# Layer 0 attention: scores on four row groups, masked into SBUF, softmax in SBUF, transposes four steps behind, one copy in three on VectorE

## The chip, the cores and the metric

The kernel runs on one NeuronCore of a Trainium2 chip. The metric is the device time of one execution in microseconds; less is better. Five engines take part: TensorE (PE; its weight loads are shown apart as PEld), VectorE (DVE), ScalarE (ACT), GpSimd (POOL) and SyncE (SP, which only issues transfers here). Each engine runs its own queue in order, and semaphores order the engines among each other.

## The reference

The model is two transformer layers with the normalisation after each block. All data is fp32. Layer 0 is grouped-query attention with 32 heads of 16 channels and 8 key/value heads, causal, on 4 sequences of 256 tokens and 512 channels, and a feed-forward product whose weight is dequantised. Layer 1 is attention with 32 heads of 128 channels and a distance bias, and a product with a weight of -1, 0 and 1.

```python
# layer 0, cut
q = (x @ Wq + bq).reshape(B, S, 32, 16).transpose(0, 2, 1, 3)
k = repeat(4, (x @ Wk + bk) as 8 heads of 16)
v = repeat(4, (x @ Wv + bv) as 8 heads of 16)
scores = einsum('bhqd,bhkd->bhqk', q, k) / sqrt(16)
scores = where(causal, scores, -1e9)
p = softmax(scores, axis=-1)
out = einsum('bhqk,bhkd->bhqd', p, v) @ Wo + bo
x = layernorm(x + out)
x = layernorm(x + x @ dequantised_weight.T + bias)
# layer 1: the same shape of block, with its own weights
```

## The kernel before

Tokens lie in eight tiles of 128. Layer 0 is one software pipeline, the function `run`. It goes over 64 steps `(b, qt, h, i)`: batch `b` (4), query tile `qt` (2), `h` (2) and `i` (4). A step is four heads of one query tile. For `qt` 0 the keys are the first 128 tokens, so the scores of a step are 128 x 4 x 128 ("first half" of a batch, eight steps); for `qt` 1 they are all 256 ("second half").

Queries and keys are held with channels on the partitions, in strips of 32: strip r holds two key/value heads of 16 channels. `kT` has two copies of the keys, in each of which one of the two heads of every strip is zeroed (index `e`), so that a matmul over the 32 partitions of a strip gives the scores of one head only. `i` counts the four query heads that share a key head.

`begin0` starts a step. It multiplies on two strips (rows 64h to 64h+63), each against both copies of the keys, into a PSUM tile of two banks; the pool `ps_s0` has two such tiles. DVE adds the causal mask in place to the 128 columns on the diagonal (L489), for all four heads at once, and takes the negated maxima over all columns (L492). ACT makes four exponentials, one a head, out of PSUM into the SBUF tile `pr`, with the row sums beside them (L276). Then `divide0` is called: the reciprocal of the sums of the step before on DVE (L281), and the division of its `pr` on POOL (L284).

Three steps later `transpose0` transposes `pr` on PE (L299), one bank for each 128 keys, and `evacuate` copies the bank to the tile `prT`. `evacuate` takes turns: one copy on DVE (L102), the next on ACT (L104). Two steps after the transposes `end0` is called. It does nothing until the last of the eight steps of a query tile; then it multiplies all the probabilities with the values (L532; 8 matmuls for `qt` 0, 16 for `qt` 1) into the bank `o`, four strips of output columns at a time, copies `o` to `oT` and appends a generator `tail0` to the list `tails`.

Between the steps, `fill` advances other work by one piece: `project0` of the next batch (transposed x, keys pk L388, queries pq L401, values pv), and the open tails: output projection py (L440) with its residual sum y (L442), normalisation with statistics on DVE and a power on POOL (L262), transposed x1, feed-forward product pf (L457), second normalisation, and the transpose into `x2T` that layer 1 reads.

[...] three in the pool `ps_w`, shared by the transposes, projections and tails; four for scores (two tiles of two); one for `o`.

The order of instructions on each engine is not the order of the calls alone: a scheduler moves independent instructions, so a score step may stand inside a block of pf or pq. Instructions marked `keep_in_program_order` are held in place.

Layer 1, from about 270 us on, is bound by PE. It uses the same `evacuate`, with alternating turns.

Of the kernel before, what the change touches and what calls it, by code (L numbers as in the profile page):

```python
# [12 lines left out]
F32 = mybir.dt.float32  # L13
# [15 lines left out]
MASKED = -3.0e38  # L29
# [32 lines left out]
def block_kernel(  # L62
# [29 lines left out]
    dram = pool(ctx, "dram", 4, space=bass.MemoryType.DRAM)  # L92

    turn = [0]
    last = []

    def evacuate(dst, src):

        if not last:
            turn[0] ^= 1  # L100
        if turn[0] and not last:
            nc.vector.tensor_copy(dst, src)  # L102
        else:
            nc.scalar.copy(dst, src)  # L104
# [31 lines left out]
    def bank_m(name):  # L136
        return ps_w.tile([P, D], F32, tag="w", name=name)
# [127 lines left out]
    def normalise(dst, y, factors):  # L265
        nc.vector.tensor_scalar(dst, y, *factors, ALU.subtract, ALU.mult)
# [8 lines left out]
    def exponentials(pr, sc, nm, sums, i, w):  # L275
        nc.scalar.activation(  # L276
            pr[:, i, 0:w], sc, AF.Exp, bias=nm[:, i : i + 1], accum_out=sums[:, i : i + 1]
        )
# [193 lines left out]

    ahead, tails = deque(), deque()

    def begin0(b, qt, h, i):

        qT, kT, _ = qkv0[b]
        w = (qt + 1) * P
        name = f"0_{b}_{qt}_{h}_{i}"
        nm, sums, pr = softmax_tiles(a0, name, 6)  # L480
        sc = ps_s0.tile([P, 2, 2, 2 * P], F32, tag="s", name=f"sc_{name}")
        for j in range(2):
            rows = slice(32 * (2 * h + j), 32 * (2 * h + j) + 32)
            nc.tensor.matmul(  # L484
                sc[:, j, :, 0:w], qT[rows, i, ts(qt, P)], kT[rows, :, 0:w], start=True, stop=True
            )
        scf = sc.rearrange("p j e k -> p (j e) k")
        diag = scf[:, :, w - P : w]
        nc.vector.tensor_tensor(  # L489
            diag, diag, causal.unsqueeze(1).to_broadcast([P, G, P]), ALU.add  # L490
        )
        nc.vector.tensor_reduce(nm, scf[:, :, 0:w], AX.X, ALU.max, negate=True)  # L492
# [12 lines left out]
        if undivided:  # L505
            divided(*undivided.pop(), True)

    def transpose0(b, qt, h, i, pr):
        name = f"0_{b}_{qt}_{h}_{i}"
        if i == 0:  # L510
            open0[h] = [
                a0.tile(
                    [P, G, 4, 4, 32], F32, tag="prT", name=f"prT0_{b}_{qt}_{h}_{kt}", bufs=5
                )
                for kt in range(qt + 1)
            ]
        transposed_probabilities(
            name,
            pr,
            [(kt, open0[h][kt][:, i].rearrange("p j n q -> p n j q")) for kt in range(qt + 1)],  # L520
        )
        return open0[0], open0[1] if h else None

    def end0(b, qt, h, i, prT):
        if (h, i) != (1, G - 1):
            return
        o = ps_o0.tile([P, G * P], F32, tag="o", name=f"o0_{b}_{qt}")
        v = qkv0[b][2]
        for kt in range(qt, -1, -1):
            for e in range(2):  # L530
                for r in (2, 3, 0, 1):
                    nc.tensor.matmul(  # L532
                        o[32 * r : 32 * r + 32, :],
                        v[:, kt, r, ts(e, 32)],
                        prT[r // 2][kt][:, :, :, 2 * (r % 2) + e, :],
                        start=(kt == qt and e == 0),
                        stop=(kt == 0 and e == 1),
                    )
        oT = a0.tile([P, G, P], F32, tag="oT", name=f"oT0_{b}_{qt}")
        evacuate(oT.rearrange("p i q -> p (i q)"), o)  # L540
        tails.append(tail0(2 * b + qt, oT))

    def before0(step):
        b, qt, h, i = step
        if (qt, h, i) == (0, 0, 0):
# [14 lines left out]
    ahead.append(project0(0))  # L560
    tails.append(feed_forward_weight())
    run(
        [(b, qt, h, i) for b in range(B) for qt in range(2) for h in range(2) for i in range(G)],
        begin0,
        transpose0,
        end0,
        before0,
        fill,
        lag=3,
        more=2,  # L570
        rest=divide0,
    )
    la.close()


# [470 lines left out]
    def fill1():  # L1046
# [16 lines left out]
        lag=1,  # L1063
# [39 lines left out]
```

## Time and profile before

| what | value |
|---|---|
| time, median of 3 runs | 961.02 us (960.78 to 964.9) |
| the profiled execution | 960.96 us, span 958.8 us |
| PE busy | 922.0 us, 96% |
| DVE busy | 619.4 us, 65% |
| POOL busy | 445.6 us, 46% |
| ACT busy | 315.2 us, 33% |
| layer 0's loop | the first score matmul starts at 13.91 us; layer 1's first product starts at 270.11 us |
| score matmuls, first half | 128 records of 32x256, mean 426 ns |
| score matmuls, second half | 128 records of 32x512, mean 638 ns |
| mask L489 | 64 of 128x512, mean 694 ns |
| maxima L492 | 32 of 128x512, mean 686 ns; 32 of 128x1024, mean 1222 ns |
| exponentials L276, layer 0 | 128 of 128x128, mean 371 ns; 128 of 128x256, mean 475 ns |
| division L284, layer 0 | 32 of 128x512, mean 1112 ns; 32 of 128x1024, mean 1907 ns |

How to read it. A row of the profile names line, engine, operation, output and inputs with shapes, then the count, the busy time, the mean of one, and the idle time of the engine before these instructions with what ended it. An fp32 matmul stands as two records, and its duration includes the pipeline's depth, so that the distance between starts tells better what it costs. A share of busy time is an average over stages; what a change in one stage is worth is read from that stage. The granted clock is that of TensorE, as a part of its full speed.

### The profile page before, as it was taken

What the parts mean: (1) busy time and instruction counts of PE and PEld (TensorE: products, weight loads), DVE (VectorE), ACT (ScalarE), POOL (GpSimd) and SP (SyncE); (2) the same over time, 40 slices, a digit from 0 to 9 for tenths busy, and PEclk for the clock granted to TensorE, in tenths of its full rate; (3) what the DMA queues carried; (4) which work ended last, traced back from release to release, by engine and by line L of the source; (5) the groups of instructions that cost most, each with busy time, mean ns of one, the idle gap of its engine ahead of it and who ended that gap; (6) DMA issues with size and microseconds to landing.
All of it is one profiled execution on the core that took longest, in us unless ns stands there. A gap on an engine that the chain in (4) does not pass through costs nothing.

```text
span 958.8 us, 11377 instructions
## 1 busy us (share of the span) xinstructions
PE 922.0 (96%) x3593; PEld 554.1 (58%) x3593; DVE 619.4 (65%) x1291; ACT 315.2 (33%) x1194; POOL 445.6 (46%) x461
## 2 busy tenths in 40 slices
PE   8999999998899999999999999999999999999996
PEld 5655455553544445666666666666666666666652
DVE  4886777778533447655667666666676576666566
ACT  3674555466411003232222222212122122214441
POOL 3563553554457015445443543534543534556732
PEclk9999999999899999999999999999999999999998
DMA  8500000000020102444443353343344333432001
GB/s 242 184 1 1 0 1 1 1 1 1 1 88 22 45 0 72 128 115 126 110 135 86 112 152 99 121 125 95 117 125 111 115 83 110 126 94 69 1 34 55
DMA packets 76418, 74.45 MB, mean 78 GB/s; under 512 B 5957, under 2 KB 52678, under 8 KB 76358
## 3 DMA queue, kind: packets, MB, share of 16 engines
q1 hardware_dynamic: 75014, 72.02, 26.2%
q10 hardware_dynamic: 1344, 1.70, 0.6%
q8 instruction: 29, 0.48, 0.2%
q14 instruction: 31, 0.25, 0.1%
HBM read 49.58 MB, written 24.12 MB: 77 GB/s over the span
## 4 chain that ended last, share of the span: by engine, by line
PE 79%; POOL 9%; DVE 6%; ACT 2%; issue 1%; DMA 1%; ACTq 0%; POOLq 0%; DVEq 0%
PE p_q L632 18%; PE po L881 14%; PE sc L968 7%; PE o L1008 7%; PE p_k L632 5%; PE p_v L632 5%; PE sc L484 4%; PE pt L299 3%; PE py L440 3%; PE pf L457 3%; PE o L532 2%; PE pq L401 2%; POOL pr L284 2%; ACT pr L276 2%; PE py L842 2%; POOL x L903 2%
## 5 line engine op out<-in xcount | busy, mean ns | idle before, releaser
L276 ACT ACTIVATE pr<-sc,nm 128x256 f32<-128x256 f32 (+1 forms) x512 | 209.5, 421 | 362.2 <-DVE nm L984 277.2
L284 POOL TENSOR_TENSOR pr<-pr,sums 128x512 f32<-128x512 f32 (+1 forms) x128 | 190.4, 1489 | 231.2 <-DVE sums L281 220.9
L976 DVE SCALAR_TENSOR_TENSOR sc<-table,sc 128x128 f32<-128x128 f32 (+1 forms) x256 | 86.1, 356 | 34.7 <-PE sc L968 32.4
L276 ACT ACTIVATION_READ_ACCUMULATOR pr<-sc,nm 128x1 f32 x512 | 104.2, 203 | 0.0
L968 PEld LDWEIGHTS sc<-kT,qT 128*128 128x128 f32 x512 | 82.3, 191 | 35.1 <-issue 29.7
L968 PE MATMUL sc<-kT,qT 128*128 128x256 f32 (+1 forms) x512 | 95.0, 327 | 0.0
L1008 PE MATMUL o<-prT,v 128*128 128x512 f32 x192 | 92.9, 592 | 0.0
L310 DVE STREAM_TRANSPOSE blocks<-pr 128x512 f32<-128x512 f32 x84 | 57.6, 698 | 45.2 <-POOL pr L284 45.1
L646 DVE TENSOR_TENSOR qT<-p_q,qT 128x512 f32<-128x512 f32 x96 | 64.6, 686 | 33.6 <-PE p_q L632 32.8
L299 PE MATMUL pt<-ident,pr 128*128 128x128 f32 x432 | 64.3, 284 | 11.7 <-POOL pr L284 8.2
L299 PEld LDWEIGHTS pt<-ident,pr 128*128 128x128 f32 x432 | 50.7, 145 | 38.1 <-issue 19.9
L984 DVE TENSOR_REDUCE nm<-sc 128x2 f32<-128x512 f32 (+1 forms) x128 | 70.1, 551 | 1.5
L484 PE MATMUL sc<-kT,qT 32*128 32x256 f32 (+1 forms) x256 | 61.6, 532 | 2.8 <-ACT pr L276 2.7
L492 DVE TENSOR_REDUCE nm<-sc 128x4 f32<-128x512 f32 (+1 forms) x64 | 61.0, 954 | 1.2
L881 PE MATMUL po<-wo,so 128*128 128x256 f32 x224 | 58.0, 381 | 2.1 <-POOL so L612 2.1
L632 PE MATMUL p_q<-x2T,ws_q 128*128 128x512 f32 x128 | 59.8, 592 | 0.0
L489 DVE TENSOR_TENSOR sc<-sc,causal 128x512 f32<-128x512 f32 x64 | 44.4, 694 | 22.8 <-PE sc L484 22.5
L104 ACT COPY o<-o 128x512 f32<-128x512 f32 x29 | 17.0, 586 | 124.9 <-PE o L1008 124.9
L632 PE MATMUL p_q<-xt,ws_q 128*128 128x512 f32 x128 | 57.7, 592 | 0.0
L881 PE MATMUL po<-wo,o 128*128 128x256 f32 x224 | 57.7, 380 | 0.0
L632 PE MATMUL p_q<-x2T,wq 128*128 128x512 f32 x128 | 57.6, 592 | 0.0
L881 PE MATMUL po<-to,so 128*128 128x256 f32 x224 | 53.3, 381 | 1.0 <-POOL so L615 1.0
(155 smaller groups left out, 1410.2 us busy)
## 6 DMA issues: line engine op xcount, KB each, us to landing
way<-blocks SPq DMA_DIRECT2D x112, 128.0 KB, 2.5
prT<-way SPq DMA_DIRECT2D x28, 512.0 KB, 3.7
wq<-in_L_attn_w_qkv_dram SPq DMA_DIRECT2D x8, 1024.0 KB, 5.1
wo<-in_L_attn_w_o_dram SPq DMA_DIRECT2D x8, 1024.0 KB, 5.1
way<-blocks SPq DMA_DIRECT2D x112, 64.0 KB, 1.8
prT<-way SPq DMA_DIRECT2D x28, 256.0 KB, 2.6
wk<-in_L_attn_w_qkv_dram SPq DMA_DIRECT2D x4, 512.0 KB, 4.1
wv<-in_L_attn_w_qkv_dram SPq DMA_DIRECT2D x2, 1024.0 KB, 6.3
```

Of the source, the lines that this page charges most:

```text
L276: nc.scalar.activation(pr[:, i, 0:w], sc, AF.Exp, bias=nm[:, i : i + 1], accum_out=sums[:, i : i + 1])
L284: nc.gpsimd.tensor_tensor(pr[:, :, 0:w], pr[:, :, 0:w], sums.unsqueeze(2).to_broadcast([P, G, w]), ALU.mult)
L299: nc.tensor.transpose(pt[:, i, :], pr[:, i, ts(kt, P)], ident)
L484: nc.tensor.matmul(sc[:, j, :, 0:w], qT[rows, i, ts(qt, P)], kT[rows, :, 0:w], start=True, stop=True)
L492: nc.vector.tensor_reduce(nm, scf[:, :, 0:w], AX.X, ALU.max, negate=True)
L632: nc.tensor.matmul(bank, fixed, moving, start=(c == 0), stop=(c == 1))
L646: add = lambda dst, a, b: nc.vector.tensor_tensor(dst, a, b, ALU.add)
L881: nc.tensor.matmul(bank[:, ts(n, HALF)], left[:, c, :], right[:, c, :], start=(c == 0), stop=(c == 1),)
L968: nc.tensor.matmul(sc[:, m, 0:w], qT[:, 2 * j + m, b * S + qt * P : b * S + (qt + 1) * P], kT[:, b * S : b * S + w], start=True, stop=True,)
L976: nc.vector.scalar_tensor_tensor(sc[:, m, 0:w], table[:, 2 * P - w :], slopes[kv * G + 2 * j + m], sc[:, m, 0:w], ALU.mult, ALU.add,)
L984: nc.vector.tensor_reduce(nm[:, 2 * j : 2 * j + 2], sc[:, :, 0:w], AX.X, ALU.max, negate=True)
L1008: nc.tensor.matmul(o, v1[:, 2 * b + kt, ts(kv, P)], prT[:, kt].rearrange("p j h q -> p h j q"), start=(kt == 0), stop=(kt == qt),)
```

## The change

A step becomes `(b, qt, e, i)`: all four strips against one copy of the keys, four matmuls with 128 or 256 columns instead of two with 256 or 512. The heads of a step are others, the number of steps and of heads in a step is the same. The four matmuls write four banks, and `ps_s0` has one such tile instead of two smaller ones.

DVE adds the mask in one instruction over the whole width and writes to SBUF, into `pr`; the mask tile has 128 columns of zeros ahead of the triangle for this. The maxima and the exponentials read `pr` in SBUF, and the exponentials are made in place.

The transposes of a step come four steps behind it instead of three. `prT` is now one tile for each `e`, with both blocks of keys, and two such tiles instead of five smaller ones. The output matmuls of a query tile are made in two blocks, after the last step of each `e`, into the same bank, which stays open between them.

In layer 0 `evacuate` gives DVE one copy in three, and ACT two; from layer 1 on they alternate again.

```diff
     turn = [0]
+    shares = [3]
...
         if not last:
-            turn[0] ^= 1
-        if turn[0] and not last:
+            turn[0] += 1
+        if turn[0] % shares[0] == 1 and not last:
             nc.vector.tensor_copy(dst, src)
         else:
             nc.scalar.copy(dst, src)
...
-    causal = wa.tile([P, P], F32, name="causal")
-    make_causal_mask(nc, causal, MASKED)
+    causal = wa.tile([P, 2 * P], F32, name="causal")
+    nc.gpsimd.memset(causal[:, 0:P], 0.0)
+    make_causal_mask(nc, causal[:, P:], MASKED)
...
-    ps_s0 = pool(la, "ps_s0", 2, space=PSUM)
+    ps_s0 = pool(la, "ps_s0", 1, space=PSUM)
...
-    def begin0(b, qt, h, i):
+    def begin0(b, qt, e, i):
...
-        sc = ps_s0.tile([P, 2, 2, 2 * P], F32, tag="s", name=f"sc_{name}")
-        for j in range(2):
-            rows = slice(32 * (2 * h + j), 32 * (2 * h + j) + 32)
+        sc = ps_s0.tile([P, 4, 4 * P], F32, tag="s", name=f"sc_{name}")
+        for r in range(4):
+            rows = slice(32 * r, 32 * r + 32)
             nc.tensor.matmul(
-                sc[:, j, :, 0:w], qT[rows, i, ts(qt, P)], kT[rows, :, 0:w], start=True, stop=True
-            )
-        scf = sc.rearrange("p j e k -> p (j e) k")
-        diag = scf[:, :, w - P : w]
+                sc[:, r, 0:w], qT[rows, i, ts(qt, P)], kT[rows, e, 0:w], start=True, stop=True
+            )
         nc.vector.tensor_tensor(
-            diag, diag, causal.unsqueeze(1).to_broadcast([P, G, P]), ALU.add
+            pr[:, :, 0:w],
+            sc[:, :, 0:w],
+            causal[:, 2 * P - w :].unsqueeze(1).to_broadcast([P, G, w]),
+            ALU.add,
         )
-        nc.vector.tensor_reduce(nm, scf[:, :, 0:w], AX.X, ALU.max, negate=True)
+        nc.vector.tensor_reduce(nm, pr[:, :, 0:w], AX.X, ALU.max, negate=True)
         for n in range(G):
-            exponentials(pr, scf[:, n, 0:w], nm, sums, n, w)
+            exponentials(pr, pr[:, n, 0:w], nm, sums, n, w)
...
-    def end0(b, qt, h, i, prT):
-        if (h, i) != (1, G - 1):
+    def end0(b, qt, e, i, prT):
+        if i < G - 1:
             return
-        o = ps_o0.tile([P, G * P], F32, tag="o", name=f"o0_{b}_{qt}")
+        if e == 0:
+            open0["o"] = ps_o0.tile([P, G * P], F32, tag="o", name=f"o0_{b}_{qt}")
+        o = open0["o"]
...
-            for e in range(2):
-                for r in (2, 3, 0, 1):
+            for r in range(4):
...
+        if e == 1:
+            oT = a0.tile([P, G, P], F32, tag="oT", name=f"oT0_{b}_{qt}")
+            evacuate(oT.rearrange("p i q -> p (i q)"), o)
+            tails.append(tail0(2 * b + qt, oT))
...
-        lag=3,
+        lag=4,
         more=2,
         rest=divide0,
     )
+    shares[0] = 2
     la.close()
```

More of the change, by code (lines that the diff above doesn't have):

```diff
@@ L473, in block_kernel @@
     ahead, tails = deque(), deque()
[L475 removed]
+    def begin0(b, qt, e, i):
         qT, kT, _ = qkv0[b]
         w = (qt + 1) * P
[L479 removed]
+        name = f"0_{b}_{qt}_{e}_{i}"
         nm, sums, pr = softmax_tiles(a0, name, 6)
[L481 to L483 removed]
+        sc = ps_s0.tile([P, 4, 4 * P], F32, tag="s", name=f"sc_{name}")
+        for r in range(4):
+            rows = slice(32 * r, 32 * r + 32)
             nc.tensor.matmul(
[L485 removed]
+                sc[:, r, 0:w], qT[rows, i, ts(qt, P)], kT[rows, e, 0:w], start=True, stop=True
             )
[L487 to L488 removed]
         nc.vector.tensor_tensor(
[L490 removed]
+            pr[:, :, 0:w],
+            sc[:, :, 0:w],
+            causal[:, 2 * P - w :].unsqueeze(1).to_broadcast([P, G, w]),
+            ALU.add,
         )
[L492 removed]
+        nc.vector.tensor_reduce(nm, pr[:, :, 0:w], AX.X, ALU.max, negate=True)
         for n in range(G):
[L494 removed]
+            exponentials(pr, pr[:, n, 0:w], nm, sums, n, w)
         divide0()
@@ L506, in divide0, with transpose0 @@
             divided(*undivided.pop(), True)
-    def transpose0(b, qt, h, i, pr):
-        name = f"0_{b}_{qt}_{h}_{i}"
+    def transpose0(b, qt, e, i, pr):
+        name = f"0_{b}_{qt}_{e}_{i}"
         if i == 0:
-            open0[h] = [
-                a0.tile(
-                    [P, G, 4, 4, 32], F32, tag="prT", name=f"prT0_{b}_{qt}_{h}_{kt}", bufs=5
-                )
-                for kt in range(qt + 1)
-            ]
+            open0["p", e] = a0.tile(
+                [P, 2, G, 4, 4, 32], F32, tag="prT", name=f"prT0_{b}_{qt}_{e}"
+            )
+        prT = open0["p", e]
         transposed_probabilities(
@@ L519, in transpose0 @@
             pr,
-            [(kt, open0[h][kt][:, i].rearrange("p j n q -> p n j q")) for kt in range(qt + 1)],
+            [(kt, prT[:, kt, i].rearrange("p j n q -> p n j q")) for kt in range(qt + 1)],
         )
-        return open0[0], open0[1] if h else None
-    def end0(b, qt, h, i, prT):
-        if (h, i) != (1, G - 1):
+        return prT
+    def end0(b, qt, e, i, prT):
+        if i < G - 1:
             return
-        o = ps_o0.tile([P, G * P], F32, tag="o", name=f"o0_{b}_{qt}")
+        if e == 0:
+            open0["o"] = ps_o0.tile([P, G * P], F32, tag="o", name=f"o0_{b}_{qt}")
+        o = open0["o"]
         v = qkv0[b][2]
         for kt in range(qt, -1, -1):
-            for e in range(2):
-                for r in (2, 3, 0, 1):
[L532 to L541, printed above, removed]
+            for r in range(4):
+                nc.tensor.matmul(
+                    o[32 * r : 32 * r + 32, :],
+                    v[:, kt, r, ts(e, 32)],
+                    prT[:, kt, :, :, r, :],
+                    start=(kt == qt and e == 0),
+                    stop=(kt == 0 and e == 1),
+                )
+        if e == 1:
+            oT = a0.tile([P, G, P], F32, tag="oT", name=f"oT0_{b}_{qt}")
+            evacuate(oT.rearrange("p i q -> p (i q)"), o)
+            tails.append(tail0(2 * b + qt, oT))
     def before0(step):
-        b, qt, h, i = step
-        if (qt, h, i) == (0, 0, 0):
+        b, qt, e, i = step
+        if (qt, e, i) == (0, 0, 0):
             if b == 0:
@@ L562, in block_kernel @@
     run(
-        [(b, qt, h, i) for b in range(B) for qt in range(2) for h in range(2) for i in range(G)],
+        [(b, qt, e, i) for b in range(B) for qt in range(2) for e in range(2) for i in range(G)],
         begin0,
```

## The prediction

> **What bounds the kernel now.** I read the windows by stage first, cut at the instants where the width of layer 0's score matmuls changes. Each of the four batches has a first half (128 keys, eight steps) and a second half (256 keys, eight steps); the last window also holds the drain of layer 0. Columns: length, then busy us and instructions of PE, PEld, DVE, ACT, POOL, then granted clock and DMA.
>
> ```profile
> 13.91:37.28 23.37, 22.29 (x133) 16.61 (x132) 19.30 (x41) 13.09 (x64) 10.23 (x9) 1.00 0.91 269
> 37.28:64.70 27.42, 26.82 (x145) 15.17 (x144) 22.44 (x40) 18.38 (x70) 16.18 (x11) 1.00 0.00 1
> 64.70:95.41 30.71, 29.74 (x165) 17.41 (x165) 22.54 (x48) 18.20 (x79) 13.70 (x14) 1.00 0.01 2
> 95.41:130.91 35.50, 33.34 (x158) 17.82 (x157) 25.78 (x46) 18.07 (x70) 17.72 (x13) 0.95 0.00 1
> 130.91:161.78 30.87, 29.91 (x164) 17.41 (x164) 22.68 (x48) 17.70 (x77) 13.63 (x13) 1.00 0.00 1
> 161.78:195.66 33.88, 31.72 (x157) 17.35 (x156) 25.78 (x46) 18.07 (x70) 17.72 (x13) 1.00 0.00 1
> 195.66:222.07 26.41, 23.89 (x141) 12.64 (x140) 20.65 (x44) 16.81 (x73) 12.74 (x11) 1.00 0.00 1
> 222.07:270.11 48.04, 41.75 (x194) 20.66 (x194) 29.07 (x52) 22.92 (x84) 21.53 (x15) 0.93 0.00 1
> ```
>
> PE is busy for over 90% of nearly every window, DVE for some 75%, ACT and POOL for about half. Layer 0's loop is PE-bound with DVE close behind. The change touches nothing after 270 us: there the two instruction orders agree, and the copies keep their engines because both kernels make the same number before.
>
> PE's busy time counts pipeline tails, so the timeline of PE comes next; the distance between starts is what an operation costs.
>
> ```profile
> 158.79 0.70 PE L484 MATMUL sc<-kT,qT 32*128 32x256 f32 x4
> 159.42 1.99 PE L401 MATMUL pq<-xT,wq 128*128 128x256 f32 x8
> 173.35 1.13 PE L484 MATMUL sc<-kT,qT 32*128 32x512 f32 x4
> 174.40 1.99 PE L401 MATMUL pq<-xT,wq 128*128 128x256 f32 x8
> ```
>
> A score step holds PE for 0.63 us with 256 columns and 1.05 us with 512. Each fp32 matmul is two records, so a step is two passes on two row groups that run together. The eight records of pq, 256 columns each, hold PE until 176.23, where the next transposes start: 1.83 us, of which some 0.1 is the load after the row groups, so 0.216 us each, or 0.84 ns a column. So a score step is 2 x 0.43 us of columns plus about 0.2 us for loading into and out of row groups (2 x 0.216 + 0.2 for the narrow one).
>
> Then the groups by form, for durations, and the waits of layer 0 (total us, times, longest).
>
> ```profile
> L489 DVE TENSOR_TENSOR sc<-sc,causal 128x512 f32<-128x512 f32 x64 | 44.4, 694 | 22.8 <-PE sc L484 22.5
> L492 DVE TENSOR_REDUCE nm<-sc 128x4 f32<-128x1024 f32 x32 | 39.1, 1222 | 0.8
> L102 DVE COPY prT<-pt 128x512 f32<-128x512 f32 x43 | 29.2, 678 | 3.1 <-PE pt L299 3.1
> L104 ACT COPY prT<-pt 128x512 f32<-128x512 f32 x53 | 31.1, 597 | 33.3 <-PE pt L299 33.3
> ```
>
> ```profile
> DVE sc L489 <- PE sc L484: 22.5, 28, 3.4
> PEld sc L484 <- ACT pr L276: 12.1, 18, 1.1
> PE pt L299 <- POOL pr L284: 6.2, 4, 2.6
> ```
>
> PE waits for the exponentials that free a score buffer, and four times for POOL's division; DVE's only long wait is for scores.
>
> **The change, part by part.**
>
> Scores on four row groups. A step's columns fall from 2 x 256 to 2 x 128, or from 2 x 512 to 2 x 256, with the loading unchanged: 0.63 becomes 0.43, 1.05 becomes 0.63. The trace shows two row groups together, and four column groups together in the output matmuls (L532, 32 records in 3.6 us), never four row groups. If they ran two by two a step would cost twice 0.43 or 0.63, which is 0.2 more than now; that is the upper end. I take four, as with the column groups: 32 x 0.20 + 32 x 0.42 = 19.8 us less PE. In the new order four steps of 64 have other work between their matmuls; I ignore them.
>
> Mask into SBUF. Second-half masks grow from 512 to 1024 elements. The reduction has 686 ns at 512 and 1222 at 1024, so a mask of 1024 takes about 694 + 536 = 1230 ns: 32 x 0.54 = +17 us DVE. First-half masks stay at 694.
>
> Reduction and exponentials from SBUF. [...]
>
> ```profile
> L984 DVE TENSOR_REDUCE nm<-sc 128x2 f32<-128x256 f32 x64 | 26.5, 418 | 0.9
> L182 DVE TENSOR_REDUCE even<-ident 128x2 f32<-128x128 f32 x1 | 0.3, 286 | 0.6 <-POOL ident masks.py:199 0.6
> L104 ACT COPY x2T<-pt_x 128x512 f32<-128x512 f32 x2 | 1.2, 586 | 3.0 <-PE pt_x L272 3.0
> L199 ACT COPY wq<-x2T 128x512 f32<-128x512 f32 x1 | 0.6, 619 | 3.4 <-DMA x2T<-in_L_attn_Wq_dram 3.4
> ```
>
> At 536/512 = 1.05 ns an element the PSUM reduction L984 leaves 150 ns fixed, the SBUF reduction L182 152: no gain. [...] I take the row: zero. [...] the rows show 619 - 586 = 33. By the row 256 exponentials cost ACT 8.5 us[...]. That speaks against the change, but ACT is busy for half of each window, and the sums it yields are needed by DVE's reciprocal only after the next mask and reduction (1.23 + 1.22 us, against 4 x 0.49 = 1.95 of exponentials). I cost it at nothing; without that cover it is 0.13 us a step, 8 us.
>
> Copies. 132 copies of layer 0 go 66:66 now, 44:88 after. DVE loses 22 x 0.68 = 15 us, ACT gains 22 x 0.60 = 13. ACT rises by some 21 us over eight windows, to about 20 us each: still below PE and DVE. A copy can stand behind a block of exponentials, and the three shared banks then hold PE; bounds 0 and 22 x 1 us. I take 2.
>
> One score buffer. The mask frees it, not the exponentials. Now step n+1 needs the exponentials of n-1: reduction 1.22 and 1.9 of ACT after that mask. After, it needs the mask of n, one step (about 3.9 us) later. So 12.1 us of waits go, and PE waits for a mask wherever DVE is behind. [...] the trace has two buffers and waits all the same. Behind a waiting score matmul PE's queue holds transposes and the py, pf and pq blocks, and behind those wait the copies and DVE's sums y. I take this coupling as a loss inside the halves below. The mask also takes its pr buffer earlier than the exponentials did; with six buffers and transposes four steps behind it was read two steps before, so zero.
>
> Output matmuls in two blocks of half the size. The same 192 records; in the drain the last block is half of 3.6 us: -1.8.
>
> Lag of four. The four waits for POOL (6.2 us) shrink; the loop runs one step more, whose only work is the drain's. I take -2 in the last batch. What is late next there is DVE. POOL's division, SP's queue and the DMAs are the same instructions; one more 128x128 memset on POOL stands before the loop under the weight loads.
>
> **The sum.** A second half (33.88 us) has 25.8 DVE: +8 x 0.54 - 3 copies x 0.68 = 28.1. PE loses 3.4, to about 28.3 of busy time. Two engines at 28 in lockstep cannot give 28; now the busier has 31.7 in 33.9. I put 31: -2.9. A first half (30.87) loses 1.6 of PE and gives DVE back about 2: 29.4, -1.5. Batch 0: first half under the loads (DMA 0.91), -0.5; second half starts shorter (27.42) with DVE at 22.4 + 2.3, -2. Batches 1 and 2: -4.4 each. Last batch: first half -1.6 and less POOL wait, -2; the 48 us: DVE +2.3 and nothing to hide it, +1, drain -1.8, less POOL wait -1. Total -0.5 - 2 - 8.8 - 2 - 1.8 = -15. Against that: copies +2, and one half-clock stretch: batches 1 and 2 run the same 158 matmul records in 35.50 and 33.88 us, with clocks 0.95 and 1.00, so one costs 1.6. -15 + 3.6 = about -12. The profiled run has 960.96 (span 958.80, 2.16 around it), level with the median of 961.02. 961 - 12 = 949.
>
> **The rivals.**
>
> A, the gain is paid back by DVE (16%): the second halves stay as long as now because DVE has 28 us in order, with waits for py, pf and POOL between. Left are 3 x 1.5 from the first halves, +3.6 against it: 960. For it: DVE's total hardly falls. Against: 8 us of DVE idle in a second half, most of it waiting for scores.
>
> B, lockstep through the single buffer (16%), slower: a mask starts only when its scores are whole, these only when the last mask is off. DVE then waits out each score step, 0.63 plus a tail of about 0.25, in 32 wide steps: 28.1 + 8 x 0.9 = 35.3 for a second half, 0 to +4 in each batch, +9 in all; first halves give -3, copies and clock +3.6: 971. It decides when PE reaches scores later than DVE reaches the mask in over half of the wide steps. Against: in the new order PE has 2 to 3 us of other work between two wide score steps on average, about what DVE has in reduction, reciprocal and next mask (2.6), so the two mostly cover each other.
>
> C, the sides fit better than I think (20%): second halves at 29, stalls gone: -5 x 3, first halves -5, last batch -5: 937.
>
> D, row groups run two by two (3%): +13 us of PE instead of -20; with the rest 966.
>
> The forecast itself has 45%; alone its range is 943 to 955. A measurement of this kernel can tell about 0.5%, 4.8 us, from no change. Faster by more: the forecast, C, a little of A: 0.66. Within: most of A and some of the forecast's upper edge: 0.18. Slower by more: B mostly, D: 0.16. Low end 934 takes in C with the copies at no cost; 966 takes in A, D and a weak B.
>
> **What would show it.** Score steps at 0.43 and 0.63 us by starts, or D. Wide masks at 1.23 us; reductions still 1222. Exponentials at about 0.51. DVE's second half at 28 us busy in a window of 31; if 34, A; if DVE waits for scores 30 us or more in all, B. The drain's output block at 1.8. Everything past layer 0 shifted alike: if the stretch from the last wide step on changes its length by over 3 us, my cut at 270 is wrong.

## The result, and the profile after

The changed kernel takes 950.1 us (median of four runs, 947.79 to 952.45); the kernel before, run beside it, 962.83 us. The ratio is 0.9875, 95% interval 0.9846 to 0.9904: 1.25% faster, 12 us. The profiled execution of the changed kernel has 951.23 us, its span 949.3 us.

The windows by stage, cut at the same events as before: the two halves of batches 1 and 2, and the last window with the drain of layer 0. Columns: length, then busy us and instructions of PE, PEld, DVE, ACT, POOL, then granted clock and DMA.

```profile
65.95:97.33 31.38, 28.96 (x198) 18.00 (x197) 21.87 (x46) 19.07 (x76) 12.85 (x13) 1.00 0.00 1
97.33:128.53 31.20, 27.95 (x185) 16.60 (x184) 27.48 (x42) 20.88 (x74) 18.19 (x13) 1.00 0.01 2
128.53:159.61 31.08, 30.04 (x201) 18.26 (x200) 22.61 (x47) 19.33 (x78) 12.98 (x13) 1.00 0.00 1
159.61:190.65 31.04, 28.16 (x185) 16.60 (x185) 27.58 (x42) 20.86 (x74) 18.08 (x13) 1.00 0.00 1
...
215.44:260.54 45.10, 38.70 (x237) 19.83 (x238) 32.32 (x54) 27.31 (x90) 22.26 (x16) 1.00 0.00 1
```

Four things stand out. The second halves of batches 1 and 2 went from 35.50 and 33.88 us to 31.20 and 31.04. The first halves did not shrink: 30.71 and 30.87 before, 31.38 and 31.08 now. The last window fell from 48.04 to 45.10 us, though the clock was halved for two stretches in it before and for none now, so its own work is no shorter. And PE, which was busy for 94% of a second half, is now busy for 90 to 91% of it. What follows layer 0 (688.9 us from its first key projection to the end) has the same length in both profiles.

Two things in this pair of profiles are not the change. The scores start 2.2 us later (16.14 against 13.91); over all profiles of this study that start lies anywhere from 13.1 to 16.5 us, with the old loop as with the new one. And the granted clock was halved in layer 0 for 10.2 us before (three stretches of 3.41 us) and for 3.4 us after (one). So I compare stage lengths with 1.7 us taken off for each such stretch, half of its length. So corrected, the way from the first score to layer 1 went from 250.9 to 242.5 us: 8.4 us less, not the 11.8 that the profiles show.

The runs say the same. Over 100 runs of the kernel before, the spans scatter by 2.0 to 2.4 us (standard deviation within a set); each span times its run's mean granted clock scatters by 1.0 to 1.3 us. This product, an estimate of the span at full clock, is 951.6 us for the kernel before (its four sets have 951.4 to 951.9) and 943.4 for the changed one: 8.2 us less, some 1.8 either way. So of the 12 us, about 8 are the loop's own, and about 4 come from a clock that was halved less (mean 0.992 before, 0.995 after). With four runs of the changed kernel the second part is the less certain, and why the clock was halved less is not shown.

PE's timeline at a wide score step (start, us, engine, line, operation):

```profile
159.61 0.71 PE L486 MATMUL sc<-kT,qT 32*128 32x256 f32 x8
160.26 0.55 PE L301 MATMUL pt<-ident,pr 128*128 128x128 f32 x3
```

From start to start the step holds PE for 0.65 us, against 1.05 before; a narrow one (145.15 to 145.61) for 0.46 against 0.63. The four row groups run together: eight records of 32x256 lie in the 0.65 us.

The groups by form (line, engine, operation, shapes, count | busy us, mean ns | idle before it, and its releaser), then the waits (us in total, times, longest):

```profile
L489 DVE TENSOR_TENSOR pr<-sc,causal 128x1024 f32<-128x1024 f32 x32 | 38.8, 1212 | 3.3 <-PE sc L486 3.1
L278 ACT ACTIVATE pr<-pr,nm 128x256 f32<-128x256 f32 x128 | 63.5, 497 | 19.8 <-DVE sums L283 19.8
L534 PE MATMUL o<-prT,v 128*32 128x512 f32 x192 | 31.2, 601 | 1.0 <-ACT prT L105 0.9
```

```profile
PEld sc L486 <- DVE pr L489: 22.1, 26, 2.5
DVE pr L489 <- PE sc L486: 10.0, 17, 1.5
PE sc L486 <- DVE pr L489: 8.6, 13, 1.5
```

The wide mask takes 1212 ns, and PE's busy time in score matmuls fell from 61.6 us (L484, both forms) to 40.8 (L486). The exponentials of 256 columns read SBUF now and take 497 ns. The row that tells where much of it went is L534: the same 192 records of the output matmuls are 31.2 us busy, and were 23.4 us in the kernel before. The waits have changed sides too. DVE waits for scores 10.0 us, before 22.5; PE waits for the mask that frees the one score buffer, 30.7 us in both rows, where before its loads waited 12.1 us and its matmuls 2.7 for exponentials.

From every PE matmul's start to the next one's start, summed by tile from the first score to the first key projection of layer 1, I get this account of layer 0 (us, half-clock stretches not taken off; a wait counts for the work that stands before it in PE's queue, so a row includes the standing that follows it). The last three columns are experiments told below.

| | before | after | all but the row groups (e9) | whole output blocks (e1) | no maximum (e10) |
|---|---|---|---|---|---|
| scores | 60.8 | 46.7 | 66.8 | 46.2 | 46.3 |
| output matmuls | 24.0 | 36.0 | 22.5 | 29.0 | 25.8 |
| transposes of probabilities | 63.0 | 55.8 | 54.9 | 58.7 | 57.6 |
| all | 256.0 | 244.3 | 250.6 | 241.4 | 238.6 |

Scores gave 14.1 us, transposes 7.2 us, and the output matmuls took 12.0 us back.

### The profile page after: what moved, and what is told of

Its sections match the earlier page's. It is cut to its first block, busy times and chain, and to the rows that moved or that the text cites. A ratio compares the mean times of both kernels' runs of the same rounds, so it can differ in the third digit from the quotient of the medians.

```text
span 949.3 us, 11860 instructions
## 1 busy us (share of the span) xinstructions
PE 906.8 (96%) x3849; PEld 554.4 (58%) x3849; DVE 623.8 (66%) x1269; ACT 333.9 (35%) x1216; POOL 444.7 (47%) x462
## 4 chain that ended last, share of the span: by engine, by line
PE 70%; DVE 12%; POOL 9%; ACT 5%; DMA 2%; issue 1%; ACTq 0%; POOLq 0%; SPq 0%; DVEq 0%
PE p_q L636 19%; PE po L885 14%; PE sc L972 7%; PE o L1012 7%; PE p_k L636 5%; PE p_v L636 5%; ACT pr L278 4%; PE py L442 3%; DVE pr L489 3%; PE pf L459 2%; DVE nm L495 2%; PE py L846 2%; POOL x L907 2%; POOL pr L286 2%; DVE prT L103 1%
## 5 line engine op out<-in xcount | busy, mean ns | idle before, releaser
L278 ACT ACTIVATE pr<-sc,nm 128x128 f32<-128x128 f32 (+1 forms) x256 | 105.0, 419 | 291.1 <-DVE nm L988 277.1
L278 ACT ACTIVATE pr<-pr,nm 128x128 f32<-128x128 f32 (+1 forms) x256 | 113.2, 444 | 39.3 <-DVE sums L283 30.2
L312 DVE STREAM_TRANSPOSE blocks<-pr 128x512 f32<-128x512 f32 x84 | 57.6, 698 | 45.2 <-POOL pr L286 45.1
L489 DVE TENSOR_TENSOR pr<-sc,causal 128x512 f32<-128x512 f32 (+1 forms) x64 | 60.5, 945 | 10.2 <-PE sc L486 10.0
L301 PE MATMUL pt<-ident,pr 128*128 128x128 f32 x432 | 59.9, 276 | 7.2 <-DVE prT L103 2.1
L495 DVE TENSOR_REDUCE nm<-pr 128x4 f32<-128x512 f32 (+1 forms) x64 | 60.7, 948 | 1.2
L301 PEld LDWEIGHTS pt<-ident,pr 128*128 128x128 f32 x432 | 48.6, 141 | 21.2 <-issue 10.1
L636 PE MATMUL p_q<-x2T,wq 128*128 128x512 f32 x128 | 57.6, 592 | 0.0
L105 ACT COPY prT<-pt 128x512 f32<-128x512 f32 x76 | 42.6, 582 | 39.5 <-PE pt L301 39.5
## 6 DMA issues: line engine op xcount, KB each, us to landing
prT<-way SPq DMA_DIRECT2D x28, 256.0 KB, 2.6
```

What stands on the lines that cost most here:

```text
L278: nc.scalar.activation(pr[:, i, 0:w], sc, AF.Exp, bias=nm[:, i : i + 1], accum_out=sums[:, i : i + 1])
L301: nc.tensor.transpose(pt[:, i, :], pr[:, i, ts(kt, P)], ident)
L489: nc.vector.tensor_tensor(pr[:, :, 0:w], sc[:, :, 0:w], causal[:, 2 * P - w :].unsqueeze(1).to_broadcast([P, G, w]), ALU.add,)
L495: nc.vector.tensor_reduce(nm, pr[:, :, 0:w], AX.X, ALU.max, negate=True)
L636: nc.tensor.matmul(bank, fixed, moving, start=(c == 0), stop=(c == 1))
```

## The experiments

Two theories stood at the start. T1: what the first halves did not gain was lost in the output matmuls, because the scheduler puts a score step behind the first output matmul of 7 of the 16 blocks. T2: VectorE, with its wider mask and the single score buffer, ate it. All ratios are against runs of the kernel before beside them (medians 960.4 to 961.1 us); the changed kernel's own is 0.9875. The clock differs between the kernels' runs too, so where it matters I give the product of span and clock beside the ratio; the table at the end has it for all but e6 and e10.

**e1, whole output blocks.** Each output matmul is issued behind the newest score step.

```
+            open0["sc"] = nc.tensor.matmul(sc[:, r, 0:w], ...)
...
+                with tc.issue_after(open0["sc"].ins):
+                    nc.tensor.matmul(o[32 * r : 32 * r + 32, :], ...)
```

> The changed kernel with one edge more: every output matmul is issued behind the newest score step, so that no score step stands between the first output matmul of a block and the rest (7 of the 16 blocks are split so in the changed kernel). Theory T1 (the missing gain is TensorE time lost where a score step splits an output block: a lone output matmul lasts 0.97 us where its share of an unsplit block is about 0.23): 7 blocks by 0.75 to 1 us are 5 to 7 us of TensorE, of which the stages bound by TensorE give back half or more: 3 to 6 us faster than the changed kernel, 944 to 947 us, the occupancy of the output matmuls from 36.0 to about 29 us. Theory T2 (VectorE, with the wide mask of 1.21 us and the single score buffer, sets the pace): TensorE only waits longer for the mask, within 1 us of the changed kernel's 950 us.

Measured: 948.27 us, ratio 0.9861 (0.9831 to 0.9891). The timelines of the same place in both kernels show what a split costs. The changed kernel:

```profile
161.46 1.05 PE L534 MATMUL o<-prT,v 128*32 128x512 f32 x2
162.44 0.71 PE L486 MATMUL sc<-kT,qT 32*128 32x256 f32 x8
163.08 1.06 PE L534 MATMUL o<-prT,v 128*32 128x512 f32 x6
164.07 0.66 PE L274 MATMUL pt_x<-ident,x 128*128 128x128 f32 x4
```

With whole blocks:

```profile
160.66 0.71 PE L486 MATMUL sc<-kT,qT 32*128 32x256 f32 x8
161.31 1.07 PE L535 MATMUL o<-prT,v 128*32 128x512 f32 x8
162.31 1.13 PE L403 MATMUL pq<-xT,wq 128*128 128x256 f32 x4
```

A single output matmul holds PE for 0.98 us, the other three for 0.99, and all four together for 1.00. The four fill four column groups at once; alone, one of them streams its two passes of 512 columns just as long. Seven splits at 1.0 us are the 7.0 us by which the output row of the account falls, and the busy time agrees:

```profile
L535 PE MATMUL o<-prT,v 128*32 128x512 f32 x192 | 23.9, 600 | 0.7 <-ACT prT L105 0.7
```

So the price of a split is shown. Its weight for the time is less than T1 said: of 7 us of PE, 2.8 come through in the span (949.25 to 946.44, with the one half-clock stretch at 56.5 us and the start of scores within 0.2 us in both). Transposes stand 2.9 us longer instead. The medians differ by 1.8 us, with intervals that overlap; they alone do not resolve it. Span times clock does: 943.4 and 940.7 us, a difference of 2.7, about 1.5 either way.

**e2, lag 3 in the changed kernel.** `lag=4` becomes `lag=3`.

> The changed kernel with the transposes three steps behind the scores, as before the change, instead of four. Its order on TensorE keeps 14 of the 16 output blocks whole (two in the last batch are split by transposes). T1: 5 splits fewer by 0.75 to 1 us, half of it on the path, minus the 2 us that the fourth step was forecast to bring in the last batch: 948 to 950 us, no slower than the changed kernel, the first halves of the batches 1 us shorter each. T2 (softmax latency and VectorE bound): a step has one period of about 2 us less for mask, maximum, exponentials and division, so transposes wait: 953 to 957 us.

Measured: 953.35 us, ratio 0.9910 (0.9874 to 0.9945), 3.3 us slower than the changed kernel by the medians, at the lower edge of what T2 said; by span times clock 1.7 us (945.1 against 943.4). T1's part is there too: the output row of the account is 31.7 us, 4.3 less, but the transposes have 64.4, 8.6 more. They wait for POOL's division. The first two rows are this kernel's, the third the changed kernel's only one:

```profile
PEld pt L301 <- POOL pr L286: 10.8, 8, 2.3
PE pt L301 <- POOL pr L286: 4.0, 4, 1.4
PEld pt L301 <- POOL pr L286: 1.7, 2, 0.9
```

So the fourth step of lag is worth more than the splits that it brings. The windows of batch 1 with lag 3:

```profile
66.17:95.38 29.21, 27.07 (x194) 16.80 (x193) 20.52 (x43) 18.62 (x75) 12.74 (x12) 1.00 0.00 1
95.38:129.38 34.00, 28.56 (x194) 17.48 (x193) 30.32 (x47) 21.73 (x75) 18.23 (x13) 1.00 0.01 1
```

With lag 3 the first half is 29.2 us, a gain of 1.5 against the kernel before, as forecast (that of batch 2, with a half-clock stretch in it, is 30.7 less 1.7), and the second stays at 34.0 in both batches. With lag 4 they are 31.4 and 31.2. Look at the counts: 194 and 194 PE instructions here, 198 to 201 and 185 in the changed kernel. With a longer lag one more step's transposes, which are twice as many for 256 keys, are left to the next window. So the first halves' missing gain is partly a matter of where the windows are cut, and a batch is what must be compared.

**e3, every second copy on VectorE.** `shares = [3]` becomes `shares = [2]`.

> The changed kernel with every second PSUM copy of layer 0 on VectorE again instead of every third: about 16 copies by 678 ns, 11 us, move from ScalarE to VectorE. T2 (VectorE bound in the second halves, 27.5 of 31 us busy): VectorE would have 29 to 30 of 31 us busy there, and most of the 11 us shows: 4 to 9 us slower, 954 to 959. T1: VectorE has slack of 3.5 us per second half and takes it: within 2 us of the changed kernel, 949 to 952.

Measured: 949.11 us, ratio 0.9871 (0.9843 to 0.9899): no difference from the changed kernel, as T1 said. VectorE's busy time rose by 10.7 us on the page (623.8 to 634.5). In the second half of batch 1 it is busy for 28.4 us instead of 27.5, and the window keeps its length, 31.0 us. This speaks against T2, and the new division of the copies brings nothing here.

**e4, lag 4 alone.** The kernel before with `lag=4`.

> The kernel before with nothing changed but the lag of the transposes, four steps instead of three. The prediction's step: 2 us less in the last batch, nothing elsewhere: 0.2% faster than before, 961 against 963 us. Rival: the lag brings nothing by itself, because transposes there do not wait for the softmax, within 0.5 us; or, if the later transposes split output blocks as in the changed kernel, up to 1 us slower (one block of eight is split in this kernel's order).

Measured: 957.34 us, ratio 0.9960 (0.9944 to 0.9976), 3.8 us faster than before by the ratio: more than forecast. The first half of the last batch gives 2.0 us (26.41 to 24.43), as forecast, and batches 1 and 2 another 1.8 (129.3 to 127.5 for both, corrected), which was not. PE's loads and matmuls of the transposes waited 15.4 us for POOL's division before (9.2 and 6.2), and 2.3 us with lag 4.

**e5, the mask alone.** The kernel before with the wide mask into SBUF; two row groups, two buffers, lag 3.

```
-        diag = scf[:, :, w - P : w]
-        nc.vector.tensor_tensor(diag, diag, causal..., ALU.add)
+        nc.vector.tensor_tensor(pr[:, :, 0:w], scf[:, :, 0:w], causal[:, 2 * P - w :]..., ALU.add)
```

> The kernel before with one part of the change alone: the mask is added over the whole width in one VectorE step that writes to SBUF, and maximum and exponentials read SBUF. Scores stay on two row groups with two score buffers, lag 3, output block whole. T2 (VectorE's time for the mask is what ate the gain): 64 masks by 0.53 us more in the wide half, 17 us of VectorE, of which a third or more shows in the second halves: 3 to 8 us slower than before, 964 to 969 us. Rival T3 (VectorE has slack, and the earlier release of the score buffers, after the mask instead of after the fourth exponential, takes away TensorE's waits for a buffer, some 2 us in a batch): 0 to 5 us faster, 956 to 961 us.

Measured: 961.98 us, ratio 1.0017 (1.0002 to 1.0031): 1.6 us slower, between the two. The clock hides a little: it is 0.990 in these runs and 0.993 in those of the kernel before beside them, and span times clock is 1.3 us lower (950.6 against 951.9). Batches 1 and 2 gain 1.4 us, and the last window loses 1.6 (46.1 against 44.5, corrected). So 17 us more of VectorE with an earlier release of the buffers come out near nothing together.

**e6, row groups without the way to SBUF.** Four row groups and one buffer, but the mask stays on the diagonal in PSUM and the exponentials read PSUM.

> The changed kernel with the scores on four row groups and one score buffer as it is, but the mask on the diagonal in PSUM and maximum and exponentials from PSUM, as before the change: the one buffer is held until the fourth exponential ends. If the single buffer binds then, a wide step is a chain of 0.65 scores, 0.69 mask, 1.22 maximum and about 1.9 exponentials, 4.7 us with issue, against about 3.9 us a step now: 32 by 0.8 us, 26 us slower than the changed kernel, some 970 to 990 us. If there is enough other work for TensorE and VectorE to turn to and the buffer does not bind: VectorE saves 17 us and the time is 945 to 950 us.

Measured: 1097.07 us, ratio 1.1413 (1.1385 to 1.1442): 147 us slower than the changed kernel, and far off the forecast of 20 to 40. A part of the chain of waits in a second half (start, us, what):

```profile
156.90 0.71 DVE sc L489
157.63 1.22 DVE nm L492
158.85 0.09 DVE sums L282
...
159.11 1.90 POOL pr L285
161.05 1.97 PE pt L300 x8
163.02 1.17 PE sc L485 x8
...
182.71 1.09 PE pt L300 x8
183.80 0.69 PE sc L485 x8
```

The chain is not the one I had written. The next scores stand in PE's queue behind transposes, these wait for POOL's division, and the division waits for a reciprocal that DVE reaches only behind the mask and the maximum of the newer step. The ring has 0.7 + 1.2 + 0.1 + 1.9 + 2.0 + 1.2 us, some 7 us a step where the changed kernel has 3.9. But the 2.0 and 1.2 stand in a stretch of half clock (granted 0.50 from 161.05 to 164.19 us); at full clock the same work has 1.1 and 0.7 (from 182.71), and the ring 5.7. The clock is halved for 150 of the loop's 394 us, in which PE is busy for 269. Half of that, up to 75 of the 147 us, is an estimate of what the clock costs; span times clock leaves 74 (1017.2 against 943.4). The rest goes with the longer ring: 1.8 us in each of 32 wide steps are 58 of it. So the one-step evacuation is no extra: it is what makes one score buffer bearable, and with that four row groups in this allocation.

**e7, lag 5 with whole blocks** (a seventh probability buffer), and **e8, whole blocks with all copies but the first on ScalarE** (`shares = [1000]`).

> The kernel with whole output blocks, its transposes five steps behind the scores instead of four, with a seventh probability buffer. The step from three to four brought 3.4 us in the kernel before and as much in the changed one. If transposes still wait for the softmax at four: another 1 to 3 us, 945 to 947 us. If the waits were gone at four: within 1 us of the kernel with whole blocks (948 us).

> The kernel with whole output blocks and all PSUM copies of layer 0 but the first on ScalarE: 32 or so copies by 678 ns, 22 us, leave VectorE, and as many by 579 ns, 18 us, go to ScalarE. T2 (masks that wait in VectorE's queue behind copies hold the single score buffer and TensorE): the 2.7 us in a batch that TensorE stands in score steps beyond their own length shrink to about 1, and the time falls by 2 to 5 us, 943 to 946 us. Rival: ScalarE, with 24 of 30 us busy, lets exponentials and copies queue behind each other, and transposes or copies come late: 1 to 4 us slower, 949 to 952 us.

Measured: e7 953.92 us, ratio 0.9931 (0.9908 to 0.9955); e8 958.56 us, ratio 0.9972 (0.9957 to 0.9986). Both lose, 5.7 and 10.3 us against e1, more than either of their forecasts allowed: e8 speaks against T2 again, though ScalarE's load rises with it, and of the lags three, four and five, four is best. Much of both losses is clock: it is 0.991 in e7 and 0.988 in e8, against 0.995 in e1. Span times clock leaves 2.8 and 3.7 us (943.5 and 944.4 against 940.7). In e7 the batches 1 and 2 hold 2.6 of it; in e8 they hold 0.9, and the first half of the last batch 3.5 (28.3 against 24.8, corrected). In both, PE waits more for the copy oT that ScalarE makes for the output projection, matmuls and weight loads together: 13.6 us in e7 and 12.1 in e8 from batch 1 on, 9.5 in e1 over the whole loop. How much of the loss that wait makes is not shown, nor why the clock was lower.

**e9, all but the row groups.** The kernel before with the mask into SBUF, lag 4 and one copy in three on VectorE.

> Everything of the change but the four row groups and what hangs on them: the kernel before with the wide mask to SBUF, lag 4 and one copy in three on VectorE, but scores on two row groups in two buffers and one output block a half. Against the changed kernel it prices the row groups with their single buffer and their two output blocks. If the parts add up (mask alone 0, lag 4 alone -3.4, copies 0): 957 to 959 us, so that the row groups bring 7 to 9 us of their 19.8 us of TensorE time. If lag 4 pays only where TensorE is bound by scores, or mask and lag work together: 950 to 954, and the row groups bring next to nothing.

Measured: 954.55 us, ratio 0.9928 (0.9899 to 0.9956), 6.9 us faster than before by the ratio, between the two forecasts. That is over half of what the whole change gives: row groups, single buffer and two output blocks add 5.1 us, and 6.4 with the blocks kept whole. By span times clock it is 4.5 and 3.9 us, and 6.6 with whole blocks. In the account, scores fall by 20.1 us from e9 to the changed kernel, close to the 19.8 that the row groups were to give (the row holds standing too), and output matmuls rise by 13.5.

**e10, no maximum.**

```
-        nc.vector.tensor_reduce(nm, pr[:, :, 0:w], AX.X, ALU.max, negate=True)
...
-            exponentials(pr, pr[:, n, 0:w], nm, sums, n, w)
+            nc.scalar.activation(pr[:, n, 0:w], pr[:, n, 0:w], AF.Exp, bias=zero, scale=0.0, ...)
```

> The kernel with whole output blocks, without the row maximum: the reductions are left out, and the exponentials multiply the score by zero with a constant bias (so the probabilities are not the reference's), at the same shape and number. It takes about 61 us off VectorE (32 by 1.21 and 32 by 0.68) and the maximum out of the chain from scores to transposes. T2 (what is left of TensorE's wait in score steps, 2.5 us or more in a batch, is VectorE coming late to the single buffer): the score steps fall to their own length, 8.7 us in a batch, the batches from 61 to 56 to 58 us, the time to 930 to 940 us. If TensorE or ScalarE bound the batches: within 3 us of 948 us.

Measured: 943.82 us, ratio 0.9824 (0.9796 to 0.9853), 4.5 us below e1 (4.9 by span times clock: 935.8), between the two forecasts. The page's first part shows that the work is gone from DVE (622.5 us in e1):

```profile
PE 899.6 (96%) x3849; PEld 551.7 (59%) x3849; DVE 570.2 (61%) x1205; ACT 332.4 (35%) x1216; POOL 444.3 (47%) x463
```

Over 50 us of DVE less bring 4.5, though PE's waits for the mask halve (loads and matmuls, 34.5 us in e1, 17.7 here). So some 5 us is what DVE's throughput and the maximum's latency are worth together in this loop, and the work taken away is three times what the change had added. As the theory of what ate the gain T2 does not hold; as a smaller share it is not excluded.

**e11, whole blocks and every second copy on VectorE**, the best of the parts together.

> The kernel with whole output blocks and every second copy on VectorE. Alone, the copies brought nothing against the changed kernel (949.1 against 950.1 us), whole blocks 1.8 us. T2 (VectorE close to binding, 27.3 of 30.5 us in the second halves): 1 to 3 us slower than whole blocks alone, 949 to 951 us. If ScalarE's copies delay the exponentials as with all copies on ScalarE: 1 to 3 us faster, 945 to 947 us.

Measured: 947.20 us, ratio 0.9850 (0.9824 to 0.9876), the lowest median of a kernel that computes all, and at the edge of the forecast that had the copies help. Against the changed kernel the intervals of the ratios overlap; batches 1 and 2 are 121.2 us in the trace against 124.7, and span times clock is 938.5 against 943.4.

**e12, mask and lag without the copies.**

> The kernel before with the wide mask to SBUF and lag 4, its copies as before (every second on VectorE). Mask alone gave 0, lag 4 alone -3.4 us, both with one copy in three on VectorE -6.4 us. If mask and lag work together (the mask frees the score buffers earlier, and only with the longer lag is there time to use it): 954 to 955 us, and the copies bring nothing. If the copies bring the rest here: 957 to 958 us.

Measured: 957.81 us, ratio 0.9969 (0.9954 to 0.9985). By the medians the copies would bring the 3.3 us between e12 and e9. By the trace they do not bring them in the loop's steady part: batches 1 and 2 take 125.6 us in both. The intervals just touch, and span times clock leaves 1.8 (949.1 against 947.3), so I leave the copies' share open. Mask and lag nearly add up there: 129.3 us before, 1.8 less with the lag, 1.4 less with the mask, 3.7 less with both. Over the whole run the mask does not pay beside the lag alone (949.1 against 947.0 by span times clock): the last window is 48.0 us with both and 45.2 with the lag, corrected.

Batches 1 and 2 in one view (us, from the first score of batch 1 to that of batch 3, less 1.7 for each half-clock stretch):

| kernel | batches 1 and 2 | ratio | mean clock | span x clock |
|---|---|---|---|---|
| before | 129.3 | 1 | 0.992 | 951.6 |
| lag 4 (e4) | 127.5 | 0.9960 | 0.991 | 947.0 |
| mask (e5) | 127.9 | 1.0017 | 0.990 | 950.6 |
| mask, lag 4 (e12) | 125.6 | 0.9969 | 0.993 | 949.1 |
| mask, lag 4, copies (e9) | 125.6 | 0.9928 | 0.994 | 947.3 |
| the change | 124.7 | 0.9875 | 0.995 | 943.4 |
| the change, lag 3 (e2) | 126.0 | 0.9910 | 0.995 | 945.1 |
| the change, even copies (e3) | 123.5 | 0.9871 | 0.996 | 942.7 |
| the change, whole blocks (e1) | 122.4 | 0.9861 | 0.995 | 940.7 |
| whole blocks, lag 5 (e7) | 125.0 | 0.9931 | 0.991 | 943.5 |
| whole blocks, copies on ScalarE (e8) | 123.3 | 0.9972 | 0.988 | 944.4 |
| whole blocks, even copies (e11) | 121.2 | 0.9850 | 0.993 | 938.5 |

The last column is the mean over a kernel's runs, with 0.4 to 1.7 us either way. The first column is one execution each, the others are all runs.

## Why the prediction was right, and where its steps were not

The forecast was 949.0 us, the measurement 950.1: the side and the size hold. The size holds by luck in part. The forecast had 13 us from the loop and 1.6 against it for one more half-clock stretch; measured are about 8 from the loop and 3 to 4 for it from the clock. By windows of the profiles (corrected; forecast in brackets): batch 0 -1.9 and -0.8 (-0.5, -2), batches 1 and 2 together -4.6 (-8.8), the first half of the last batch -1.6 (-2), the last window +0.5 (-1.8). Of batch 0's first half nothing is gained in the end, for its scores started 2.2 us later and ended 0.4 us later.

- *Score steps.* Forecast 0.43 and 0.63 us, measured 0.46 and 0.65. Rival D, row groups two by two, is out. The 19.8 us are there: 20.8 in PE's busy time, 18.2 by the starts (32 x 0.17 + 32 x 0.40).
- *Second halves at 31, DVE 28 busy in them.* Measured 31.0 to 31.2, with 27.5 to 27.6.
- *First halves, -1.5 each.* They kept their length. Per batch I had -4.4, measured -2.3 (129.3 to 124.7 over two), and -3.5 with whole blocks (e1). The step that failed is "The same 192 records" for the output matmuls, together with the sentence that four score steps have other work between their matmuls and can be ignored. I looked inside the score steps and not inside the output blocks, where the order puts a score step behind the first matmul of seven blocks. Term by term: output matmuls were costed at 0 in the loop and -1.8 in the drain; they cost +12.0 us of PE in all. The splits are 7.0 of it, and 2.8 of these come through in the time (e1). About 1 more is the price of smaller blocks: unsplit, 8 records hold PE for 1.00 us and 16 for 1.85, where 32 held it for 3.57. The other 4 are standing in front of the work that follows the blocks; what causes it is not shown.
- *Drain, -1.8.* The last block came as forecast, 1.92 us for 3.64, but the last window is 0.5 us longer. The wide mask costs 1.6 there (e5), where I had 1, and the rest is not traced.
- *Lag of four, -2 in the last batch.* There it was 2.0, and 1.8 more in batches 1 and 2 (e4). I had counted the four waits of the transposes for POOL's division, 6.2 us, and not the 9.2 us that their loads waited for it. This term was too small, and with the clock it stood in for the part that the output blocks took: of the 12 us, all but the row groups bring 6.9 (e9).
- *Clock, +1.6.* I expected one more half-clock stretch. The profile has two fewer, 3.4 us by the half, and the runs' clock rose from 0.992 to 0.995, some 3 us of 955. This was luck; nothing in my argument gave it.
- *Copies, +2.* No difference in the changed kernel (e3).
- *Wide mask.* 1230 ns forecast, 1212 measured. *Reductions from SBUF:* 1222 ns before, 1214 now (1024 elements); the row was right. *Exponentials from SBUF:* 497 ns against 475 and 391 against 371, +22 and +20, where the row said 33; the reads of the sums that follow each went from 206 to 188 ns, so that almost nothing is left. Costing them at nothing held: DVE's reciprocal waits for exponentials 4.8 us in all.
- *The single buffer* was given no price of its own. PE's waits for the buffer went from 14.8 to 30.7 us, 22.1 of them in the weight load, which can lie beside the matmul before (from 128.53 to 159.61 us PE is busy for 30.04 us and PEld for 18.26, in 31.08). Rival B, DVE waiting out the score steps, did not come: DVE waits 10.0 us in all. (B's 0.9 us a step would be an estimated 0.83 by the trace: a mask that waited starts 0.78 us after the first score of its wide step, 97.33 to 98.11, and scores that waited start 0.05 us after the mask ends, at 180.93.) But a single buffer is dear where it is not freed early (e6, +147 us, about half of it clock). The price is far above the 10 us that B named, and by another way: the wait goes round through POOL's division and PE's queue.
- *Rival A* had the DVE pay the gain back. e3, e5 and e10 say not by much: 10.7 us more of DVE cost 0, 17 us more cost 1.6 by the ratio and nothing by span times clock, and over 50 us less give 4.5.

What stays open is why PE still stands for 24 us of the loop in e1 (217.4 of 241.4 us busy). The chain of waits of e1 in a second half runs, with pieces left out, like this:

```profile
167.08 2.79 PE pf L459 x6
...
172.45 1.49 DVE x L268
...
174.54 1.14 DVE pr L489
...
177.02 2.08 ACT pr L278 x8
...
180.09 3.71 PE py L442 x8
```

It passes through every engine: a PE block, the norm in DVE's queue with POOL in its middle, then mask, maximum and exponentials behind it in the same queue, a copy on ACT behind the exponentials, and PE's next block. No engine is full in it (in the half from 158.23 to 188.49 us, PE and DVE are busy for 27.4 of 30.3 us each, ACT for 21.1 and POOL for 18.1), which fits with the small effect of each engine's load in e3, e8 and e10. That this ring is what holds the loop is read from one profile and not tested.

## What to carry to other kernels

When a step's work is halved on its bounding engine, look in the new instruction order for what is now put between instructions that used to run side by side: here one matmul of a block over four column groups took as long as all four (0.98 and 1.00 us), so a step in its middle doubled the block. With a shorter bounding engine, lag and order can weigh as much as an engine's load: here one step of lag gave 3.8 us and whole blocks 2.7, over 50 us less of VectorE 4.5. Compare whole periods then, not windows cut where the lag moves work across the cut. Where runs carry their granted clock, compare span times clock too: it moved the ranking of e5, e7 and e8. And a forecast that meets the time can do so with terms that are wrong both ways: run the parts.

## What the runs showed of the hardware that I had not expected

- One matmul of one column group, two passes of 512 columns, holds TensorE for 0.98 us; three hold it for 0.99 and four for 1.00.
- In layer 0 the granted clock was halved in stretches of 3.41 us or a multiple (3.41 and 6.83 us before, 3.41 after). The profiles here but e6 had one to five units of 3.41 us in it, at other places each time; e6 had 150 us in all, with TensorE busy for 68% of the loop, against 89 to 95% in the others. These stretches make much of the spread between runs: span times granted clock scatters half as much as the span over 100 runs of one kernel (1.0 to 1.3 us against 2.0 to 2.4).
- VectorE's maximum reads SBUF hardly faster than PSUM (1214 and 1222 ns for 1024 elements, 682 and 686 for 512), and ScalarE's exponentials read it 20 to 22 ns slower, with the read of the sums 18 ns shorter.
